# Inner products of each strip ahead of the outer ones, and one shifted input copy loaded from DRAM

## Chip, cores and metric

The kernel runs on one core of one Trainium2 chip. The metric is the device time of one launch in microseconds. The program is written with a scheduling layer: it allots the buffers and puts each engine's instructions in a fixed order when the program is built.

## What is computed

`reference` has two layers on an input of 4 images, 96 channels, 128 x 128 pixels. The first is a state-space block and isn't touched here. The second is an attention convolution:

```python
xr, x1, x2 = _relu_split_norm(x, sc1, sc2, res_coef, nc1, nc2)
# _attn_conv(x1, x2, aw1, aw2, aw3):
key = _unfold_nonoverlap(_conv2d(x1, aw1, pad), K)      # 3 x 3 convolution, 96 -> 96
qry = _unfold_nonoverlap(_conv2d(x2, aw2, pad), K)
attn = softmax(einsum('bckl,bqkl->bqck', key, qry) / sqrt(C * kk))
value = _conv2d(x1, aw3, pad)
y1 = _layer_norm(per image: _conv2d(value, attn))       # the attention is a 3 x 3 filter
y2 = _layer_norm(_conv2d(x2, w_conv2, 1)) * x1
out = x + xr + conv1x1([y1, y2], w_full) + b_full
```

So each image needs two pairs of 3 x 3 convolutions (the maps: `x1` with two filter sets, `x2` with two), a softmax, and a 3 x 3 convolution of the value with the attention filter.

## The kernel before

**Stages.** Up to about 3670 us the program does the state-space block and the maps of image 0. From there on it alternates, for images 0 to 3, between map stages (`attention` with `img.mapped` false, images 1 to 3) and value stages (all four images). The image is cut into strips of 12 rows (`AR`), eleven in all. Beside this main stream runs a light one: the norm and split of the next image and the output of the image before. `co_run` interleaves the two in the order of emission by costs that the generators yield.

**A convolution as products.** Along a row, four output pixels are made from six input planes (a minimal filtering scheme with the points 0, 1, -1, 2, -2 and infinity), so a strip needs six matrix products, numbered 0 to 5. Products 1 to 4 are the inner ones, 0 and 5 the outer ones. Planes are stored in DRAM in that form (`x1p`, `x2p`, `vp`), and loaded pair by pair: `PAIRS` (L1361) says which two planes make a tile, and the order of the tiles. The contraction runs over 96 channels x 3 rows. It is cut into three parts:

- `ya` (L1910): a loaded tile of 128 partitions, 96 channels of the upper row and the last 32 channels of the next one; eight buffers, three tiles a strip, loaded two strips ahead (`load`, L1898).
- `yb` (L1937): 64 channels shifted by one row on partitions 0 to 63, and by two rows on 64 to 127. Both halves are ScalarE copies of `ya` (L1938), three tiles of two copies for each strip, four buffers, made one strip ahead (`turn`, L1926).
- `yc` (L1918): the last 32 channels by two rows for products 1 and 3. The other products read theirs out of `ya`.

`products` (L1456) issues TensorE's work. `main(to, i)` puts the parts `ya` and `yb` of product i into PSUM (L1477), `rest` adds the 32-channel parts (L1492). A PSUM tile `two` holds two products; the pool has three buffers of two banks, and the transposes (L1770) and the key-query products (L1645) of the map stages use the same three. The order of one call is: main of 0 and 5 into one tile, `rest`, `outer`; main of 1, 3, 2, 4 into two tiles, `rest`, `sums`. After each `main` one entry of the list `fill` is called (a `yb` copy, a load, or both), then `later.tick()` emits what was put off.

`outputs` (L1531) makes the evacuation. `outer` copies the outer tile to SBUF on ScalarE (`ends`, L1550, two buffers). `sums` copies the tile of products 1 and 3 (`odd`, also L1550, one buffer). One tick later `combined` runs on VectorE: four sums and differences of the odd tile with the second tile (L1564 to L1567: two into `wide` in SBUF, two in place in PSUM), then four outputs (L1572) and, between them, the addition of `ends` (L1570). The second tile is read until the last of these.

A call for 128 output channels has 384 columns for a product. In a map stage each strip has, for each of the two inputs, such a call and one in which two half strips of 64 output channels stand side by side; in a value stage a strip has one call of 96 output channels. That is 132 + 44 = 176 calls and 110 strips of inputs.

At the end of a map stage `weights` (L1683) works off the last transposes and makes the softmax. The last call of `products` is held back and drawn from it piece by piece (`self.rest`): three pieces before the last transposes, two beside the softmax, the others after it.

Of the kernel before, what the change touches and what calls it, by code (L numbers as in the profile page):

```python
# [9 lines left out]
F32 = mybir.dt.float32  # L10
BF16 = mybir.dt.bfloat16
AF = mybir.ActivationFunctionType
ALU = mybir.AluOpType
# [58 lines left out]
def kernel(  # L72
# [1287 lines left out]

    PAIRS = ((0, 5), (1, 3), (2, 4))  # L1361
    PAIR = {i: k for k, pair in enumerate(PAIRS) for i in pair}
# [93 lines left out]
    def products(ps, jobs, ws, later, evac, threes=False, fill=()):  # L1456
# [42 lines left out]

        outer, sums = evac  # L1500
        fill = iter(fill)
# [6 lines left out]
        a = pairs_of(ps)  # L1508
        to = {0: a[:, 0], 5: a[:, 1]}
        for i, _ in TWO:  # L1510
            main(to[i], i)
            beside()
            later.tick()
            yield 1.3 * share
        rest(1, TWO, to)
        outer(a)
        later.tick()
        yield 0.4 + 0.4 * share
        a, b = pairs_of(ps), pairs_of(ps)
        to = {1: a[:, 0], 3: a[:, 1], 2: b[:, 0], 4: b[:, 1]}  # L1520
        for i, _ in FOUR:
            main(to[i], i)
            beside()
            later.tick()
            yield 1.3 * share
        rest(0, FOUR, to)
        sums(a, b)
        later.tick()
        yield 0.4 + 0.6 * share

    def outputs(pool, m, n, parts, later, then):  # L1531

        got = []

        def at(v, k):
            if isinstance(v, list):
                return v[k]  # L1540
            if len(v.shape) == 4:
                return v[:, :, k]
            return v.rearrange("p h (t k) -> p h t k", k=TW)[:, :, :, k]

        def rows(v):
            return v.rearrange("p (h t) -> p h t", t=TN)

        def copy_of(x, name, bufs):
            t = pool.tile([128, 2, AR * TN], F32, name=name, bufs=bufs)[:m, :, :n]
            nc.scalar.copy(t, x[:m, :, :n])  # L1550
            return t

        def outer(c):
            later(lambda: got.append(copy_of(c, "ends", 2)))

        def sums(a, b):
            def first():
                t = copy_of(a, "odd", 1)
                later(lambda: combined(t))

            def combined(t):
                w = pool.tile([128, 2, AR * TN], F32, name="wide", bufs=1)[:m, :, :n]
                ends, v = got[0], b[:m, :, :n]
                nc.vector.tensor_sub(w[:, 1], t[:, 1], v[:, 1])  # L1564
                nc.vector.tensor_add(w[:, 0], t[:, 1], v[:, 1])
                nc.vector.tensor_sub(v[:, 1], t[:, 0], v[:, 0])  # L1566
                nc.vector.tensor_add(v[:, 0], t[:, 0], v[:, 0])  # L1567
                for k, j, f in ((1, 1, AA), (2, 0, AA * AA), (0, 0, 1.0), (3, 1, AA**3)):
                    if k == 0:
                        nc.vector.tensor_add(v, ends, v)  # L1570
                    for p, e, o in parts:
                        nc.vector.scalar_tensor_tensor(  # L1572
                            at(o, k), rows(w[p:e, j]), f, rows(v[p:e, j]), ALU.mult, ALU.add
                        )
                later(then)

            later(first)

        return outer, sums

# [11 lines left out]
    class Taps:  # L1592
# [4 lines left out]
        def __init__(self, ps, later, pool, slots, taps):  # L1597
            self.ps, self.later, self.pool, self.slots = ps, later, pool, slots
            self.taps = [(k, min(k + taps, KK)) for k in range(0, KK, taps)]
            self.sm = pool.tile([C, KK, C], F32, name="sm")  # L1600
            self.rings = [pool.tile([128, 3, slots, PW], F32, name=f"ring{i}") for i in range(2)]
            for t in self.rings:
                nc.gpsimd.memset(t[:, :, :, 0:1].rearrange("p r i w -> p (r i) w"), 0.0)
            self.groups, self.todo, self.rest = 0, [], ()

# [77 lines left out]
        def weights(self):  # L1683
# [3 lines left out]
            self.later.flush()  # L1687
            for _ in range(3):
                yield next(rest, 0.0)
# [13 lines left out]
            yield 4.0  # L1703
            for _ in range(2):
                yield next(rest, 0.0)
# [15 lines left out]
    class PairTaps(Taps):  # L1721
# [3 lines left out]
        def __init__(self, ps, later, pool):  # L1725
# [8 lines left out]
            for t in self.rings:  # L1734
                for j in range(TW):
                    nc.gpsimd.memset(t[:, :, :, JB * j + TN : min(JB * (j + 1), JW)], 0.0)
            self.todo, self.rest = [], ()

# [144 lines left out]
    class Attention:  # L1883
# [3 lines left out]
        def __init__(self, ps, p1, p2, pm):  # L1887
# [5 lines left out]
            for b in range(1, NB):  # L1893
                self.todo += [(b, m, c) for c in self.chunks for m in (0, 1)]
                self.todo += [(b, 2, c) for c in self.chunks]
            self.raw, self.cols, self.c = {}, {}, 0

# [28 lines left out]
        def turn(self, c):  # L1926
# [8 lines left out]
            def copy(h, k):  # L1935
                if h == 1:
                    yb.append(self.p2.tile([128, 2, AR * TN], F32, name="yb", bufs=4))  # L1937
                nc.scalar.copy(  # L1938
                    yb[k][64 * h - 64 : 64 * h, :, :n], ya[k][0:64, :, h * TN : h * TN + n]
                )  # L1940

            return [lambda h=h, k=k: copy(h, k) for k in range(3) for h in (1, 2)]

        def begin(self):
            for c in (0, 1):
                for k in range(3):
                    self.load(c, k)
            for f in self.turn(0):
                f()
# [748 lines left out]
```

## Time and profile before

| | |
|---|---|
| median of 3 runs | 6409.91 us (6400.53 to 6413.18) |
| profiled execution, its own time | 6409.68 us |
| its span | 6407.8 us |
| busy: PE, DVE, ACT, POOL | 5253.4, 4699.9, 3759.4, 3238.6 us |
| bytes moved by DMA | 1205.30 MB, mean 188 GB/s |
| from 3670 us on (2738 us): PE, DVE, ACT, POOL busy | 2301.2, 1997.1, 1454.8, 935.8 us |

PE is TensorE's matmul, PEld its weight load, DVE is VectorE, ACT ScalarE, POOL GpSimd, SP the engine that issues most DMAs. A row of the waits reads "engine, tile and line that waited <- engine, tile and line that it waited for: total us, times, longest us". A row of the groups gives line, engine, operation, output <- input, shape, count, then busy us and mean ns, and the idle time ahead of it with what ended it. A row of the stage table gives a stretch in us and, for each engine, its busy us in it with the count of instructions. PEclk is the granted share of TensorE's full clock.

### The profile page before, as it was taken

How to read it: one execution, taken by the hardware profiler on the slowest of the kernel's cores; microseconds unless marked ns; L12 is line 12 of the kernel's file. 1: busy time of each engine (PE TensorE's matmuls, PEld its weight loads, DVE VectorE, ACT ScalarE, POOL GpSimd, SP SyncE). 2: the span in 40 equal slices, each digit the busy share in tenths (PEclk: the TensorE clock that was granted, in tenths of full speed). 3: DMA queues.
4: the chain of work that ended last, by engine and by line, in shares of the span. 5: the costliest groups of instructions: out<-in, count | busy, mean ns of one | idle time of the engine just before them, and what ended most of it. 6: DMA issues, size and time to landing. Idle time of an engine off the chain costs nothing. (4 is left out here: it accounts for less than half of the span.)

```text
span 6407.8 us, 76468 instructions
## 1 busy us (share of the span) xinstructions
PE 5253.4 (82%) x23264; PEld 2254.8 (35%) x23264; DVE 4699.9 (73%) x7132; ACT 3759.4 (59%) x4770; POOL 3238.6 (51%) x2476
## 2 busy tenths in 40 slices
PE   6889988987888643989988588977888877889888
PEld 2333322322222111444433234345333444345553
DVE  4247878988989768989844686468774687988767
ACT  1247767787787666777622465466644665545642
POOL 1326757978879554979822234436304365022310
PEclk9899989998999765999999799989989888999989
DMA  6766777775675766676667686665776656967668
GB/s 155 175 160 189 198 199 199 214 221 163 198 202 171 202 183 207 196 213 179 182 185 195 166 228 163 195 169 156 214 199 184 175 149 165 245 167 180 191 168 221
DMA packets 897706, 1205.30 MB, mean 188 GB/s; under 512 B 230644, under 2 KB 745642, under 8 KB 884816
## 3 DMA queue, kind: packets, MB, share of 16 engines
q1 hardware_dynamic: 866640, 1145.36, 65.5%
q0 software_dynamic: 16336, 38.51, 2.3%
q10 hardware_dynamic: 14320, 16.54, 0.9%
q8 instruction: 187, 3.06, 0.2%
q14 instruction: 223, 1.83, 0.1%
HBM read 777.82 MB, written 345.62 MB: 175 GB/s over the span
## 5 line engine op out<-in xcount | busy, mean ns | idle before, releaser
L633 PE MATMUL bank<-y,wp 128*128 128x512 f32 (+3 forms) x3584 | 1310.9, 622 | 83.8 <-DMA y<-y 41.0
L866 POOL TENSOR_TENSOR y<-y,dl 128x1024 f32<-128x1024 f32 x384 | 1058.5, 2757 | 263.0 <-DVE dl L858 240.3
L833 POOL TENSOR_TENSOR dl<-dl,u 128x1024 f32<-128x1024 f32 x384 | 1008.8, 2627 | 253.1 <-ACT dA L809 121.1
L854 DVE TENSOR_TENSOR_SCAN dA<-dA,pBC 128x512 f32<-128x512 f32 x768 | 981.6, 1278 | 30.7
L2169 PE MATMUL bank<-y,wn 128*64 128x384 f32 (+5 forms) x2408 | 680.1, 507 | 58.3 <-DMA y<-x1d 34.1
L1477 PE MATMUL two<-ya,wd 128*64 128x192 f32 (+3 forms) x2376 | 582.2, 414 | 174.0 <-ACT odd L1550 65.1
L633 PEld LDWEIGHTS bank<-y,wp 128*128 128x128 f32 (+3 forms) x3584 | 456.2, 168 | 749.3 <-issue 651.1
L858 DVE TENSOR_TENSOR dl<-dA,pBC 128x512 f32<-128x512 f32 x768 | 528.5, 688 | 255.8 <-PE pBC L747 183.8
L747 PE MATMUL pBC<-xr,wbc 60*128 60x512 bf16 (+1 forms) x1536 | 457.8, 404 | 311.5 <-DVE dA L854 239.1
L1938 ACT COPY yb<-ya 64x768 f32<-64x768 f32 (+1 forms) x660 | 537.7, 815 | 195.5 <-PE two L1477 113.8
L676 ACT ACTIVATE dl<-pd,dtb 128x512 f32<-128x512 f32 x768 | 485.5, 684 | 187.9 <-PE pd L747 171.5
L1477 PE MATMUL two<-yb,wd 128*64 128x192 f32 (+3 forms) x2376 | 559.0, 400 | 4.0 <-ACT yb L1938 4.0
L837 DVE TENSOR_TENSOR pBC<-dl,pBC 128x512 f32<-128x512 f32 x768 | 527.5, 687 | 8.8 <-POOL dl L833 7.8
L2169 PEld LDWEIGHTS bank<-y,wn 128*64 128x64 f32 (+3 forms) x2408 | 310.3, 169 | 357.2 <-issue 186.2
L809 ACT ACTIVATE dA<-dl,negA 128x1024 f32<-128x1024 f32 x384 | 420.3, 1141 | 2.3
L1477 PEld LDWEIGHTS two<-ya,wd 128*64 128x64 f32 (+1 forms) x2376 | 262.2, 165 | 370.9 <-ACT odd L1550 75.0
L676 ACT ACT_TABLE_LOAD x248 | 318.2, 1283 | 91.9 <-PE pd L747 79.7
L747 PEld LDWEIGHTS <-wbc 60*128 60x128 bf16 (+1 forms) x1536 | 103.1, 96 | 752.1 <-issue 739.3
L1477 PEld LDWEIGHTS two<-yb,wd 128*64 128x64 f32 (+1 forms) x2376 | 289.7, 167 | 150.5 <-issue 42.1
L1477 PE MATMUL two<-ya,wa 128*96 128x384 f32 (+1 forms) x528 | 231.2, 521 | 72.9 <-DMA ya<-vp 27.0
L1550 ACT COPY odd<-two 128x384 f32<-128x384 f32 (+5 forms) x176 | 115.8, 658 | 291.3 <-PE two L1492 179.1
L1406 POOL TENSOR_TENSOR pl<-x 96x256 f32<-96x256 f32 (+3 forms) x396 | 275.2, 710 | 0.0
(322 smaller groups left out, 9105.4 us busy)
## 6 DMA issues: line engine op xcount, KB each, us to landing
u<-zb SPq DMA_DIRECT2D x192, 1024.0 KB
yms<-y SPq DMA_DIRECT2D x96, 512.0 KB
xn<-xnew SPq DMA_DIRECT2D x128, 384.0 KB
ya<-vp SPq DMA_DIRECT2D x120, 336.0 KB
y<-y SPq DMA_DIRECT2D x128, 258.2 KB
zb<-z SPq DMA_DIRECT2D x64, 512.0 KB
y<-yms SPq DMA_DIRECT2D x64, 512.0 KB
ya<-x1p SPq DMA_DIRECT2D x90, 336.0 KB
```

Of the source, the lines that this page charges most:

```text
L633: nc.tensor.matmul(blocks(pz[p:e]), lhsT=ws[k][:, d, c : c + e - p], rhs=window(ys[k], at, d, n), start=(i == 0), stop=(i == len(terms) - 1),)
L676: nc.scalar.activation(dst, src, AF.Softplus, bias=bias)
L747: nc.tensor.matmul(p, lhsT=w[rows], rhs=xr[rows, at : at + CH], start=True, stop=True)
L809: nc.scalar.activation(live[m]["dA"], live[m]["dl"], AF.Exp, scale=negA[:, g % 3, k : k + 1])
L833: nc.gpsimd.tensor_mul(t, t, u_view(n))
L837: nc.vector.tensor_mul(p, live[n]["dl"][:, bass.ts(half, CH)], p)
L854: nc.vector.tensor_tensor_scan(h, h, p, init, ALU.mult, ALU.add)
L858: nc.vector.tensor_mul(live[n]["dl"][:, sl], live[n]["dA"][:, sl], live[n]["C", half])
L866: nc.gpsimd.tensor_add(v, v, t.rearrange("p (a b) -> p a b", b=W))
L1477: nc.tensor.matmul(of(to[p:e], r), lhsT=w[:, i, c : c + e - p], rhs=tiles(t[k][PAIR[i]][:, SLOT[i]], o, r), start=(k == 0), stop=False,)
L1938: nc.scalar.copy(yb[k][64 * h - 64 : 64 * h, :, :n], ya[k][0:64, :, h * TN : h * TN + n])
L2169: nc.tensor.matmul(pc[p:e, :n].rearrange("p (h w) -> p h w", w=W), lhsT=w[:, c : c + e - p], rhs=v[:, :, 0:W], start=(i == 0), stop=(i == ...
```

## The change

Three things change. (1) In `products` the four inner products come first; the second tile is requested only when product 2 needs it; the outer ones follow. `PAIRS` is put in the same order, so that the inner planes are loaded and copied first. (2) `outer` and its copy go. `sums` writes all four sums and differences to one SBUF tile (`sums`, twice the size of `wide`) with two instructions of full width and makes outputs 1 and 2; `ends`, called after the outer products, adds the outer tile in PSUM to the sums and makes outputs 3 and 0. (3) In the room of the `ends` tiles a tile `yd` (two buffers) takes the place of the third `yb` tile: its partitions 64 to 127 are loaded from DRAM two strips ahead (`load_direct`), the other half is still a ScalarE copy. `yb` has three buffers now. The pieces of the held-back call are split (2, 3) around the softmax, where they were (3, 2). In the built program ScalarE has 440 `yb` and 110 `yd` copies (660 `yb` before) and no `ends` copies, VectorE has 352 instructions fewer, SP 110 DMAs more; TensorE's count is the same.

```diff
-    PAIRS = ((0, 5), (1, 3), (2, 4))
+    PAIRS = ((1, 3), (2, 4), (0, 5))
...
-        outer, sums = evac
+        sums, ends = evac
...
+        a = pairs_of(ps)
+        to = {1: a[:, 0], 3: a[:, 1]}
+        for i, _ in FOUR:
+            if i == 2:
+                b = pairs_of(ps)
+                to |= {2: b[:, 0], 4: b[:, 1]}
+            main(to[i], i)
+            beside()
+            later.tick()
+            yield 1.3 * share
+        rest(0, FOUR, to)
+        sums(a, b)
+        later.tick()
+        yield 0.4 + 0.6 * share
         a = pairs_of(ps)
         to = {0: a[:, 0], 5: a[:, 1]}
         for i, _ in TWO:
...
         rest(1, TWO, to)
-        outer(a)
+        ends(a)
         later.tick()
         yield 0.4 + 0.4 * share
-        a, b = pairs_of(ps), pairs_of(ps)
-        to = {1: a[:, 0], 3: a[:, 1], 2: b[:, 0], 4: b[:, 1]}
-        for i, _ in FOUR:
...
+        def out(k, x, f, y):
+            for p, e, o in parts:
+                nc.vector.scalar_tensor_tensor(
+                    at(o, k), rows(x[p:e]), f, rows(y[p:e]), ALU.mult, ALU.add
+                )
...
             def combined(t):
+                u = pool.tile([128, 2, 2, AR * TN], F32, name="sums", bufs=1)[:m, :, :, :n]
+                v = b[:m, :, :n]
+                nc.vector.tensor_sub(u[:, :, 1], t, v)
+                nc.vector.tensor_add(u[:, :, 0], t, v)
+                out(1, u[:, 1, 1], AA, u[:, 0, 1])
+                out(2, u[:, 1, 0], AA * AA, u[:, 0, 0])
+                made.append(u)
...
+        def ends(c):
+            def closed():
+                if not made:
+                    later(closed)
+                    return
+                u, v = made[0], c[:m, :, :n]
+                nc.vector.tensor_add(v, u[:, 0], v)
+                out(3, u[:, 1, 1], AA**3, v[:, 1])
+                out(0, u[:, 1, 0], 1.0, v[:, 0])
                 later(then)
...
             def copy(h, k):
-                if h == 1:
-                    yb.append(self.p2.tile([128, 2, AR * TN], F32, name="yb", bufs=4))
+                if k == 2:
+                    yb.append(self.direct.pop(c))
+                elif h == 1:
+                    yb.append(self.p2.tile([128, 2, AR * TN], F32, name="yb", bufs=3))
...
-            return [lambda h=h, k=k: copy(h, k) for k in range(3) for h in (1, 2)]
+            fill = [lambda h=h, k=k: copy(h, k) for k in range(3) for h in (1, 2)][:5]
+            return [*fill, lambda: self.load_direct(c + 1)]
+
+        def load_direct(self, c):
...
+            i0, i1 = PAIRS[2]
+            t = self.direct[c] = self.p2.tile([128, 2, AR * TN], F32, name="yd", bufs=2)
+            src = src_of[0:64, slice(i0, i1 + 1, i1 - i0), r0 + 2 : r0 + 2 + r]
+            nc.sync.dma_start(
+                t[64:128, :, : r * TN], src.rearrange("c i h t -> c i (h t)")
+            )
```

More of the change, by code (lines that the diff above doesn't have):

```diff
@@ L1515, in products @@
         rest(1, TWO, to)
-        outer(a)
+        ends(a)
         later.tick()
         yield 0.4 + 0.4 * share
-        a, b = pairs_of(ps), pairs_of(ps)
-        to = {1: a[:, 0], 3: a[:, 1], 2: b[:, 0], 4: b[:, 1]}
-        for i, _ in FOUR:
[L1522 to L1529, printed above, removed]
     def outputs(pool, m, n, parts, later, then):
-        got = []
+        made = []
         def at(v, k):
@@ L1546, in rows @@
             return v.rearrange("p (h t) -> p h t", t=TN)
[L1548 to L1554, printed above, removed]
+        def out(k, x, f, y):
[3 more added lines that the diff above has]
+                )
@@ L1556, in sums @@
         def sums(a, b):
             def first():
-                t = copy_of(a, "odd", 1)
+                t = pool.tile([128, 2, AR * TN], F32, name="odd", bufs=1)[:m, :, :n]
+                nc.scalar.copy(t, a[:m, :, :n])
                 later(lambda: combined(t))
             def combined(t):
-                w = pool.tile([128, 2, AR * TN], F32, name="wide", bufs=1)[:m, :, :n]
-                ends, v = got[0], b[:m, :, :n]
-                nc.vector.tensor_sub(w[:, 1], t[:, 1], v[:, 1])
@@ L1565, in combined @@
[L1565 to L1574, printed above, removed]
+                u = pool.tile([128, 2, 2, AR * TN], F32, name="sums", bufs=1)[:m, :, :, :n]
@@ new lines, in combined @@
+                v = b[:m, :, :n]
[4 more added lines that the diff above has]
+                made.append(u)
+            later(first)
+        def ends(c):
[7 more added lines that the diff above has]
+                out(0, u[:, 1, 0], 1.0, v[:, 0])
@@ L1575, in combined @@
                 later(then)
-            later(first)
-        return outer, sums
+            later(closed)
+        return sums, ends
     def by_threes(v, r):
@@ L1603, in __init__ @@
                 nc.gpsimd.memset(t[:, :, :, 0:1].rearrange("p r i w -> p (r i) w"), 0.0)
-            self.groups, self.todo, self.rest = 0, [], ()
+            self.groups, self.todo, self.rest, self.held = 0, [], (), (3, 2)
         def flat(self, m):
@@ L1687, in weights @@
             self.later.flush()
-            for _ in range(3):
+            for _ in range(self.held[0]):
                 yield next(rest, 0.0)
@@ L1703, in weights @@
             yield 4.0
-            for _ in range(2):
+            for _ in range(self.held[1]):
                 yield next(rest, 0.0)
@@ L1736, in __init__ @@
                     nc.gpsimd.memset(t[:, :, :, JB * j + TN : min(JB * (j + 1), JW)], 0.0)
-            self.todo, self.rest = [], ()
+            self.todo, self.rest, self.held = [], (), (2, 3)
         def flat(self, m):
@@ L1895, in __init__ @@
                 self.todo += [(b, 2, c) for c in self.chunks]
-            self.raw, self.cols, self.c = {}, {}, 0
+            self.raw, self.cols, self.direct, self.c = {}, {}, {}, 0
         def load(self, c, k):
@@ L1940, in copy @@
                 )
-            return [lambda h=h, k=k: copy(h, k) for k in range(3) for h in (1, 2)]
+            fill = [lambda h=h, k=k: copy(h, k) for k in range(3) for h in (1, 2)][:5]
+            return [*fill, lambda: self.load_direct(c + 1)]
+        def load_direct(self, c):
+            if c >= len(self.todo):
+                return
+            b, m, (r0, r) = self.todo[c]
+            src_of = (imgs[b].x1p, imgs[b].x2p, imgs[b].vp)[m]
+            r = (r + 2) // 3 * 3
+            i0, i1 = PAIRS[2]
[4 more added lines that the diff above has]
+            )
         def begin(self):
@@ L1947, in begin @@
                     self.load(c, k)
+            self.load_direct(0)
             for f in self.turn(0):
```

## The prediction

> **What bounds the kernel now.** I read the stage table first, then TensorE's waits, then the groups of instructions, and the timeline last. The change touches only the last part of the run, from 3670 us on, where `Attention` works: eleven strips for each value product (four stages) and eleven strips for each pair of maps (three stages). Busy time by stage (the columns are PE, PEld, DVE, ACT, POOL, the granted TensorE clock, the DMA share and GB/s):
>
> ```profile
> 3670.00:3830.00 160.00, 125.80 (x402) 52.04 (x403) 135.02 (x222) 107.82 (x141) 61.80 (x83) 0.88 0.88 234
> 3830.00:4650.00 820.00, 686.31 (x4004) 359.02 (x4002) 563.39 (x1144) 474.30 (x665) 360.90 (x519) 0.92 0.67 180
> ...
> 4900.00:5480.00 580.00, 469.29 (x2913) 265.79 (x2913) 419.41 (x836) 335.47 (x478) 277.12 (x401) 0.88 0.64 170
> 5480.00:5640.00 160.00, 139.71 (x443) 58.49 (x443) 141.06 (x180) 81.21 (x94) 0.00 (x0) 0.94 0.87 234
> 5640.00:6190.00 550.00, 485.56 (x3223) 288.39 (x3219) 418.56 (x665) 288.14 (x363) 166.34 (x239) 0.94 0.66 176
> ```
>
> TensorE is busy 81 to 88% of the map stages (second, third and last row); no other engine passes 77% there. Over all 2738 us PE is busy 2301 and idle 437. Its work is one ordered stream, so a microsecond of its idle time is a microsecond of the run unless another wait takes its place. What ended that idle time:
>
> ```profile
> PE two L1477 <- ACT odd L1550: 80.3, 37, 10.1
> PE two L1477 <- ACT kt L1775: 43.0, 31, 3.7
> PE two L1477 <- ACT ends L1550: 28.4, 19, 3.4
> PE two L1477 <- DMA ya<-vp: 27.0, 1, 27.0
> PE two L1645 <- ACT odd L1550: 25.0, 15, 6.3
> ...
> PE two L1477 <- ACT yb L1938: 23.4, 15, 3.6
> PE two L1645 <- DVE ring L1572: 19.0, 10, 5.6
> ...
> PE two L1770 <- ACT odd L1550: 13.6, 9, 3.3
> ```
>
> Read these as waits for a PSUM buffer: a matmul that starts a new `two` tile waits until the tile that last held the slot has been read out. Summed by releaser over all rows: `odd` copies 119 us in 61 waits, `ends` copies 30, `kt` copies 49, VectorE's last outputs (L1572) 47, `yb` copies 23 (an input, not a slot). By stage `odd` is 49 us in 3830 to 4650, 44 in 4900 to 5480, 9 in 5640 to 6190 and 18 in the four value stages together.
>
> The copies take under 0.8 us; they cost TensorE because ScalarE comes to them late:
>
> ```profile
> ACT ends L1550 <- PE two L1492: 232.4, 79, 7.8
> ...
> ACT odd L1550 <- PE two L1492: 179.1, 52, 9.5
> ...
> ACT yb L1938 <- PE two L1477: 113.8, 63, 11.9
> ```
>
> ScalarE executes in order. While it stands at an `ends` or a `yb` copy whose TensorE work isn't done, nothing behind it runs, and it then also has the norm and split instructions of the next image ahead of the `odd` copy. At 4304.2 to 4310.5 one such case is open in the timeline: TensorE idles 6.3 us, while ScalarE works through two activations and two `yb` copies before `odd` at 4310.02, and VectorE still holds the previous product's second tile until its L1572 of 4310.89.
>
> [...] `plv<-diff` (L1406, both inputs SBUF, 96x256) has a median of 414 ns but a mean of 558 and a maximum of 2782, while L1572, with one PSUM input, has 548 and at most 557 for the `ring` shape. [...] after the idle 27.04 us at 3681.63 pairs of matmuls start 1.28 us apart, later 0.64. [...]
>
> **Part by part.** The sum is made against the profiled execution: span 6407.8, its own time 6409.68, the median of the runs 6409.91; they differ by less than I can resolve, so I count from 6410.
>
> *Copies removed (ScalarE).* 176 `ends` copies, busy 115.8 us, and one `yb` copy in six: 110 x 0.815 us = 90 us. 206 of 1455 us in the window. ScalarE is not the bound, so this is worth only what it takes off TensorE's waits. Its 232 us of standing at `ends` go too, and the wait of the third pair's copy for a slot.
>
> *VectorE.* Four differences and sums of half width become two of full width: [...] Against that, two of the four output instructions (L1572) now read two SBUF tiles. The bound below is 0 (no GpSimd at work, as in 5480 to 5640, POOL 0.00); above, the mean excess of L1420, mean 688 less median 417 = 0.27 us, on 132 map products x 2 = 71 us. I take 0.2 us, 53 us. VectorE is a wash; nothing gained or lost on the path.
>
> *PSUM slots.* This decides. In the order of the built program (map stages) the old sequence is ends-tile, odd-tile, second tile, then transposes: 26 of 44 second tiles start on the slot whose `ends` copy was issued just two matmul groups before, and the tile behind the four inner products often takes the odd slot with only a transpose or product of 2 to 3 us between. In the new one, for 40 of 44 products of the first map stage, the odd slot is next taken by a transpose or a product of transposes that stands behind the two outer products (about 3.3 us in these stages), and the second tile is released after two VectorE instructions (1.9 us), not nine (about 5.3 us). But the outer tile is now released by VectorE (add and two outputs, 0.96 + 2 x 0.55 = 2.1 us), not by ScalarE in 0.8 us, and second tiles come round sooner. In the value stages 10 of 11 outer tiles take the odd slot directly, so a wait of one copy stays.
> Map stages: `odd` and `ends` are 117 us of waits; I let a third remain: -76. Value stages: 32 us become 38 direct reuses x 0.65 us = 25: -7. `yb`: half of 23: -10. Waits for VectorE: 47 become 60: +13. Bounds: nothing of the 172 us goes (and +40 for VectorE comes), or all of it.
>
> *The new load.* 110 loads of 64 x 2 x 384 floats, 197 KB, 21 MB. The page's first queue took 65.5% of 16 x 6407.8 us for 866640 packets, 77.5 ns each; at one packet a row (an estimate) a load is 128 x 77.5 / 16 = 0.62 us of all engines. In a map stage that is hidden under a share of 0.67; in a value stage 11 x 0.62 = 6.8 us are 4 points on 0.88. The tile is filled two strips ahead, so its cover is a whole strip (12 us and more); if the cover were gone each value stage would lose up to 7 us, 27 in all. The load waits on SP until the outer products of strip c, which still read the slot that strip c + 2 is to have, are done. Behind it stand the stores of `oc`, the next `ya` loads and the light work's loads. SP already stands 231 us at the `yc` load (L1921) for the same place in TensorE's stream; with the inner products first that wait ends earlier, and the new one ends where the old one did. Between 0 and 2 us each (231/110); I take +8 us for loads and queue together.
>
> *Order of the rest.* In `weights` the held-back product now gives three pieces to the softmax gap instead of two, and one accumulating tile stays in PSUM during the last transposes: within 3 us either way, three times, 0. At the end of the run the last evacuation is four VectorE instructions shorter: 3.5 us of the chain 6356.2 to 6360.2 shrink by about 2: -2.
>
> *Clock.* From the stage table idle 11.7% goes with clock 0.94, 16.3% with 0.92, 19.1% with 0.88. 74 us less idle on 1950 us of map stages are 4 points; bounds 0 and 4 points of clock on 1641 busy us (60 us, if clock followed idle one for one). I take -11.
>
> Sum: -76 - 7 - 10 + 13 + 8 - 2 - 11 = -85 us: 6325.
>
> **Rivals.** (1) *The lateness is not ScalarE's.* What delays `odd` is the light work's chain: ScalarE waits 75 us for VectorE's `half`, 54 for `mq`, 75 for TensorE's `bank`. Then `odd` stays late, only `ends` (-30) and `yb` (-10) go and new waits give 20 back: 6390. For it: the 10.1 us maximum. Against: most waits are 1 to 3 us, in reach of the added slack.
> (2) *VectorE becomes the releaser that is late* (slower). Two of three tiles of a product are now freed by VectorE, the busiest evacuator (337 of 420 us in 5060 to 5480), whose queue is shared with the split. At 4303 us it was a whole product behind. Savings before new waits are 106 us; so it decides from 106/132 = 0.8 us of new wait per map product, against 47/176 = 0.27 now. At 1.2 us: 158 - 106 = +52: 6462. For it: slots of second tiles are reused 3 tiles later where it was 5. Against: release work falls from 5.3 to about 2 us.
> (3) *All the slot waits go* and the clock follows: -172 - 40: 6200.
> (4) *The change doesn't do it*: excluded; the built program has 440 + 110 copies for 660, no `ends`, 110 new loads, and the same 16953 TensorE instructions.
>
> **How the numbers follow.** Forecast (6255 to 6385) 0.60; rival 3 and anything below 6255 0.10; rival 1 (6385 to 6423) 0.13; rival 2 above 6423 0.17. A difference under about 0.2% (13 us) can't be told from none, so of rival 1 a third counts as faster. Faster 0.74, same 0.09, slower 0.17. The range 6250 to 6435 leaves out about 0.1 on each side.
>
> **What would show it.** Right: no `ends`; TensorE's waits for `odd` near 50 us; its waits for VectorE outputs near 60; VectorE's busy time within 20 us; ScalarE about 206 us less; PEclk up 1 to 2 points in the map stages. Wrong: waits for `sums`, `two` or outputs of VectorE above 150 us (rival 2), `odd` still over 100 (rival 1), or waits for DMA `yd` at all.

## The result

The changed kernel takes 6489.39 us (median of 6 runs, 6485.9 to 6507.95) against 6400.65 us of the kernel before (6 runs, 6377.87 to 6413.18): a ratio of 1.0159, 95% interval 1.0141 to 1.0177. It is slower by about 1.6%, where the forecast said faster by 1.3%, and it lies above the range. (The two medians alone give 1.0139, 89 us: the kernel before took 6401 us here and 6396 to 6412 us beside the runs below, so a difference between runs that were not made together is uncertain by some 0.2%.) The profiled execution took 6487.49 us, its span is 6485.7 us; the clock is 0.897 where it was 0.902.

Of the busy time, the forecast was nearly right: VectorE 4690.2 us (9.7 less), ScalarE 3560.2 us (199 less), GpSimd 3250.7 us. TensorE is the one that differs: 5296.3 us for the same instructions (43 more). The stage table, from the first product of each stage to the first of the next (columns as in the forecast: PE, PEld, DVE, ACT, POOL, clock, DMA share, GB/s); here the second map stage, the value stage after it, the last map stage and the sum of all seven, of the kernel before:

```profile
4632.20:5430.00 797.80, 647.66 (x3678) 335.34 (x3676) 555.34 (x1043) 421.54 (x582) 329.99 (x458) 0.88 0.64 174
5430.00:5612.10 182.10, 164.56 (x503) 67.10 (x503) 153.94 (x198) 93.74 (x109) 5.70 (x16) 0.95 0.90 241
5612.10:6195.30 583.20, 510.19 (x3313) 300.04 (x3314) 446.31 (x706) 301.88 (x378) 166.34 (x239) 0.94 0.67 178
...
sum 2726.20, PE 2301.19 PEld 1180.58 DVE 1993.62 ACT 1453.38 POOL 934.62; mean PE 328.74 PEld 168.65 DVE 284.80 ACT 207.63 POOL 133.52
```

and of the changed one:

```profile
4641.10:5478.70 837.60, 666.85 (x3678) 340.23 (x3676) 557.51 (x944) 376.39 (x511) 329.99 (x462) 0.86 0.62 170
5478.70:5672.80 194.10, 173.13 (x503) 68.86 (x503) 154.67 (x189) 81.47 (x94) 4.88 (x11) 0.92 0.88 236
5672.80:6269.20 596.40, 522.40 (x3317) 306.90 (x3318) 424.64 (x616) 253.84 (x309) 162.09 (x239) 0.92 0.65 177
...
sum 2817.60, PE 2347.23 PEld 1197.33 DVE 1985.12 ACT 1255.22 POOL 946.38; mean PE 335.32 PEld 171.05 DVE 283.59 ACT 179.32 POOL 135.20
```

All seven stages together are 91 us longer. That is 13 more than the span's 78, because the first value stage began 13.5 us earlier than before and ended at the same time. TensorE is busy 46 us longer and idle 45 us longer (470 against 425). The clock records of the two traces have only two values, full and half; in this part the clock stood at half for 575 us, where it had been 487. The second map stage alone gives 40 us. TensorE's waits over the whole of this part, in the changed kernel:

```profile
PE two L1477 <- DVE own L1553: 41.9, 22, 7.7
PE two L1477 <- issue: 39.6, 22, 5.3
PE two L1477 <- ACT odd L1560: 38.9, 34, 3.3
...
PE two L1477 <- DMA yd<-x2p: 26.2, 4, 10.0
...
PE two L1653 <- ACT odd L1560: 24.4, 8, 13.0
PE two L1778 <- DVE sums L1567: 22.8, 11, 6.0
PE two L1778 <- ACT odd L1560: 19.8, 13, 6.7
PE two L1477 <- DVE sums L1567: 19.4, 10, 5.0
...
PE two L1477 <- DVE ring L1553: 15.0, 9, 3.3
```

Of ScalarE's releases, `odd` has gone from 119 to 83 us, `ends` from 30 to 0, the input copies from 23 to 9. But VectorE's releases (`sums`, and the tiles of outputs `own` and `ring`) are 110 us where they were 47, the load is waited for 26 us, and 48 us have no releaser that the profile shows ("issue", here and in a smaller row), against 3 before. The waits have not gone; they have changed their owner.

### The profile page after: what moved, and what is told of

It is laid out like the page before. It is cut to its first block, busy times and chain, and to the rows that moved or that the text cites. A ratio compares the mean times of both kernels' runs of the same rounds, so it can differ in the third digit from the quotient of the medians.

```text
span 6485.7 us, 76017 instructions
## 1 busy us (share of the span) xinstructions
PE 5296.3 (82%) x23264; PEld 2268.6 (35%) x23264; DVE 4690.2 (72%) x6780; ACT 3560.2 (55%) x4484; POOL 3250.7 (50%) x2476
## 5 line engine op out<-in xcount | busy, mean ns | idle before, releaser
L1477 PE MATMUL two<-ya,wd 128*64 128x192 f32 (+3 forms) x2376 | 587.9, 417 | 134.7 <-ACT kt L1783 34.8
L1948 ACT COPY yb<-ya 64x768 f32<-64x768 f32 (+1 forms) x440 | 358.3, 814 | 154.0 <-PE two L1477 74.2
L1477 PEld LDWEIGHTS two<-ya,wd 128*64 128x64 f32 (+1 forms) x2376 | 268.8, 168 | 326.9 <-issue 129.2
L1477 PE MATMUL two<-yb,wd 128*64 128x192 f32 (+2 forms) x1584 | 379.4, 406 | 0.4 <-ACT yb L1948 0.4
L1477 PE MATMUL two<-ya,wa 128*96 128x384 f32 (+1 forms) x528 | 237.0, 534 | 110.5 <-DMA wa<-watd 27.2
L1566 DVE TENSOR_TENSOR sums<-odd,two 128x384 f32<-128x384 f32 (+5 forms) x176 | 137.1, 779 | 216.0 <-ACT odd L1560 187.0
```

Of the source, the lines that this page charges most:

```text
L1477: nc.tensor.matmul(of(to[p:e], r), lhsT=w[:, i, c : c + e - p], rhs=tiles(t[k][PAIR[i]][:, SLOT[i]], o, r), start=(k == 0), stop=False,)
L1948: nc.scalar.copy(yb[k][64 * h - 64 : 64 * h, :, :n], ya[k][0:64, :, h * TN : h * TN + n])
```

## Taking the change apart

Each run is given by its ratio to the kernel before in the runs of the same chip. The changed kernel is 1.0159; 0.0010 is 6.4 us. First the load and the outer tile. In the first run ScalarE makes all six copies again:

```diff
-            fill = [lambda h=h, k=k: copy(h, k) for k in range(3) for h in (1, 2)][:5]
-            return [*fill, lambda: self.load_direct(c + 1)]
+            return [lambda h=h, k=k: copy(h, k) for k in range(3) for h in (1, 2)]
...
-            self.load_direct(0)
```

> The changed kernel with all six shifted copies on ScalarE again and no load of its own for the third pair; inner products first and the uncopied outer tile stay. If VectorE as the late releaser costs the time (theory A), nothing is gained back: 6475 to 6500 us, with some 110 us of TensorE's waits on VectorE's sums and outputs. If the load does (theory B: 26 us of TensorE's waits for it, 48 us of issue, a fuller SP queue), most of the 89 us come back: 6400 to 6430. If it is the order of the pieces (theory C), 6475 to 6500 as well.

1.0058 (1.0045 to 1.0070), 6450.72 us. The time lies in none of the expected ranges. Without the load the kernel is 0.0101 faster, 65 us by the ratios (39 between the medians, but the kernel before took 6411 us beside this run and 6401 beside the changed kernel); the rest of the change costs 0.6%. Neither theory A nor B holds alone. Next, in addition, the outer tile is copied by ScalarE:

```diff
         def ends(c):
+            t = pool.tile([128, 2, AR * TN], F32, name="ends", bufs=1)[:m, :, :n]
+
+            def copied():
+                nc.scalar.copy(t, c[:m, :, :n])
+                later(closed)
...
-                u, v = made[0], c[:m, :, :n]
+                u, v = made[0], t
...
-            later(closed)
+            later(copied)
```

> As the run without the load, and the outer tile is copied to SBUF by ScalarE again, so that ScalarE and not VectorE releases its slot; inner products are still first, and the second tile is still released after two full-width VectorE sums. Theory A, if the outer tile is the slot that matters: 6390 to 6430. Theory B: the same as without the load, within 15 us, or slower by the copies. Theory C (the order as such): as slow as the changed kernel or slower, 6480 to 6520.

1.0045 (1.0028 to 1.0061), 6440.04 us: not to be told from the run above. The value stages do show what the forecast's second rival named. In the third of them, without the load:

```profile
PE two L1477 <- DVE own L1553: 14.9, 9, 2.6
PE two L1477 <- ACT odd L1560: 3.9, 4, 1.2
```

and with the outer tile copied by ScalarE:

```profile
PE two L1477 <- ACT ends L1578: 6.6, 7, 2.0
PE two L1477 <- ACT yb L1952: 5.1, 4, 1.3
```

Over the four value stages the wait for VectorE's `own` is 42 us in the first run, under 1 us in the second and 3 us in the kernel before, and the four are 687, 662 and 669 us long. So there VectorE as the releaser of the outer tile seems to cost what ScalarE's copy didn't; the two programs also differ in the order of their instructions, which matters below, so this is a reading. The map stages are 2077, 2079 and 2057 us long. But the profiled run of the second kernel is its fastest by 22 us (6416.25; the others 6438.9 to 6453.81), and the median keeps 11 us of the gain.

Then the load on the side of the kernel before, and its control, which makes the room for it by one buffer less for `ends` (the load's lines are those of the change):

```diff
-            later(lambda: got.append(copy_of(c, "ends", 2)))
+            later(lambda: got.append(copy_of(c, "ends", 1)))
```

> The kernel before with only the load of the third pair's shifted copy to a tile of its own added (yb in 3 buffers, ends in 1 for the room); outer products first, outer tile copied by ScalarE, sums as they were. Theory B: 6450 to 6490, with waits of TensorE for the load. Theory A and C: 6380 to 6405, since 90 us of ScalarE's work go and nothing else does.

> The kernel before with one buffer for the copied outer tile where it had two: the control for the runs that need the room. All theories: within 15 us of before, 6390 to 6420; if it is slower by more, the runs with one buffer have to be read against this one.

1.0202 (1.0182 to 1.0222) with the load, 1.0149 (1.0129 to 1.0168) without: with the load the kernel is 36 us slower here too, though 110 copies go. Both are slower than any theory expected. The control was the surprise, 95 us for one buffer. ScalarE's waits give it a plain reason, a copy that stands until VectorE has added the last one:

```profile
ACT odd L1550 <- PE two L1492: 241.3, 74, 8.0
ACT ends L1550 <- DVE two L1570: 184.2, 54, 12.8
```

It is not needed for most of the loss, as a run with both buffers below shows.

## Is it the load's traffic?

Four smaller edits of the changed kernel and its relatives. In the first the load is made in the map stages alone; in the value products ScalarE fills the same tile with the copy `last`:

```diff
+            def end():
+                if self.todo[c][1] == 2:
+                    last()
+                self.load_direct(c + 1)
...
             t = self.direct[c] = self.p2.tile([128, 2, AR * TN], F32, name="yd", bufs=2)
+            if m == 2:
+                return
```

> The changed kernel with the third pair's load made only in the map stages; in the value products ScalarE copies it into the same tile, so the buffers are the same. If the load costs what its bytes cost on the DMA engines of the value stages (44 loads, 24 us between the runs with and without the load): 6460 to 6470, with the value stages 20 to 27 us shorter together than in the changed kernel and the map stages as there. If it costs through the SP queue or TensorE's waits for the tile in the map stages: 6480 to 6495. If VectorE as the late releaser were behind all of it: no change, 6485 to 6495.

1.0142 (1.0116 to 1.0168). The value stages of the profiled run are 21 us shorter together (691 us), as expected, but the map stages are 21 us longer, though nothing was edited in them (the profiled run is the slowest of the five, 11 us above their median). Next, the closing addition one step later, and the numbers of held pieces put back:

```diff
-            later(closed)
+            later(closed, 1)
```

```diff
-            self.todo, self.rest, self.held = [], (), (2, 3)
+            self.todo, self.rest, self.held = [], (), (3, 2)
```

> The changed kernel with the closing addition and its two outputs put into VectorE's stream one step later, so that VectorE stands less at it while TensorE still works on the outer products. If standing at the closing addition (81 us) is what delays what VectorE does behind it: faster by 10 to 30 us, 6460 to 6480. If what decides is when the outer tile comes free: slower by 10 to 40, 6500 to 6530. If neither lies on the path: within 10 us of 6489.

> The changed kernel with the numbers of held pieces around the softmax of the second class put back from (2, 3) to (3, 2). The forecast put this part at nothing within 3 us; all theories: within 10 us of 6489. If it is off by more, the placing of single pieces alone moves the time by so much, and differences of that size between other kernels are not to be explained.

1.0140 (1.0117 to 1.0162) and 1.0177 (1.0153 to 1.0200). Neither is to be told from 1.0159, though the second median, 6507 us, misses the expected 10 us around 6489. Moving the closing addition (L1580), at which VectorE stands 81 us, brings nothing, and the held pieces are worth nothing that shows.

Then the load without any use: six copies on ScalarE as in the first run, and a load of the same bytes into a tile that nobody reads, in the value stages alone (the lines below) or in the map stages alone (`m == 2` there). The tile takes the room that the first run leaves free:

```diff
+            if m != 2:
+                return
...
+            t = self.p2.tile([128, 2, AR * TN], F32, name="yd", bufs=1)
```

> The changed kernel without its load, six copies on ScalarE (6451), and a load of the same bytes in the value stages alone into a tile that nobody reads: nothing waits for it, and no buffer or copy changes. If what the load costs in the value stages is the traffic on the DMA engines: 6465 to 6480, the value stages 15 to 25 us longer together. If it was a wait or a buffer: 6445 to 6456.

> The same with the unread load in the map stages alone. If traffic is behind the 20 to 50 us that the map stages lose with the load: 6465 to 6490. If it was the waits for the tile, the three buffers of yb or the placing: 6445 to 6460, as the DMA share is 0.62 to 0.68 there.

In the value stages, where the DMA engines were busiest (share 0.80 to 0.87, with the load 0.86 to 0.92), it costs nothing: 1.0069 (1.0050 to 1.0088) against 1.0058. In the map stages, with a share of 0.6 to 0.7, it costs 0.8%: 1.0137 (1.0115 to 1.0159), above even the range that was expected of traffic. That is the wrong way round for traffic, and nothing waits for this load.

What it does change is found in the built programs. Counted from them, without the load itself, 707 of VectorE's instructions and 480 of TensorE's stand out of the order of the kernel without load once the unread load is in the map stages (the fewest that would have to be moved to restore it). With the unread load in the value stages, which cost nothing, they are 72 and 42; with the changed kernel's own load, 730 and 598. On TensorE an instruction of the light work (norm, split and output of other images) stands on average 14 matmuls of the main stream later, and 40 or more for one in twenty; with the changed kernel's own load it is the same 14. The scheduling layer chose another order because the load was there; that it goes by its own estimate of when each instruction can start is likely, but not shown.

## Order against load

So the order was taken from one kernel and imposed on the other: for each engine, a list of the positions of all instructions from the end of the state-space block on, and a dependency without a semaphore from each to the next.

```diff
+    def pin(keep):
+        for text in PINNED.values():
+            raw = zlib.decompress(base64.b85decode(text))
+            at = 0
+            row = []
+            for d in struct.unpack(f"<{len(raw) // 2}h", raw):
+                at += d
+                row.append(keep[at])
+            for a, b in zip(row, row[1:]):
+                assert a.engine == b.engine
+                tc.add_manual_dep(
+                    b,
+                    a.name,
+                    mybir.DependencyInfo(
+                        mybir.DependencyClass.NoSync, mybir.DependencyReason.DATA
+                    ),
+                    reason="order of another build",
+                )
...
     drain(last.after(psl))
+    keep = [i for j, i in enumerate(traced()) if j >= begun and j not in set(marks)]
+    pin(keep)
```

`marks` holds the loads, which stay free (in the list for the third run below, the 110 copies that the load replaces are left out).

> The kernel with the unread load in the map stages (6496), but with the instructions of every engine in the order that the scheduling layer chose for the kernel without that load (6451); only the loads stand between SP's others. If the load costs through the order that it makes the layer choose: 6440 to 6462. If the bytes, or SP's time for them, cost the 45 us: 6485 to 6500.

> The kernel without the load (6451), with the instructions of every engine in the order that the layer chose for the kernel with the unread load in the map stages (6496). If the order costs the 45 us: 6482 to 6500, with no load at all. If the bytes do: 6440 to 6460.

| | no load | unread load in the map stages |
|---|---|---|
| order chosen without the load | 1.0058 (1.0045 to 1.0070) | 1.0073 (1.0051 to 1.0095) |
| order chosen with the load | 1.0125 (1.0104 to 1.0146) | 1.0137 (1.0115 to 1.0159) |

Down a column the order changes and costs 0.0067 and 0.0064, some 42 us; along a row the load changes and costs 0.0015 and 0.0012, less than the intervals can tell from nothing. Two of the four kernels carry an imposed list and two don't, so the list itself costs nothing that shows either. For this load the order is the cause, and it works with no load in the program at all.

The traces show one place. In the second map stage, TensorE's waits for `odd` at a key-query product (L1653; L1854 and L1855 in the two kernels with a list, whose lines are moved by it). First the old order, without and with the load:

```profile
PE two L1653 <- ACT odd L1560: 9.9, 5, 5.7
```

```profile
PE two L1854 <- ACT odd L1761: 8.6, 4, 4.8
```

and the new order without a load:

```profile
PE two L1855 <- ACT odd L1762: 15.9, 2, 12.5
```

A single wait of 12.5 us. The changed kernel has the same hole, 13.0 us, at 5093.9 us; it is 13.0 in the kernel with the unread load as well, and there is none like it in the three that have the old order (the third of them follows below), where the longest of these waits is 5.7 us. The timeline around it in the changed kernel, ScalarE's lines and the matmul that waited (start, duration, instruction):

```profile
5094.32 0.82 ACT L1948 COPY yb<-ya 64x768 f32<-64x768 f32 x1
5095.04 1.06 ACT L1154 ACTIVATE xz<-xr 96x1024 f32<-96x1024 f32 x1
...
5096.09 1.23 ACT L1147 ACTIVATE xr<-xn,shift,rstd 96x1024 f32<-96x1024 f32 x1
...
5098.60 1.24 ACT L1147 ACTIVATE xr<-xn,shift,rstd 96x1024 f32<-96x1024 f32 x1 [1.18 <-DMA xn<-xnew]
...
5104.12 1.23 ACT L1147 ACTIVATE xr<-xn,shift,rstd 96x1024 f32<-96x1024 f32 x1
...
5106.39 0.46 ACT L1560 COPY odd<-two 128x384 f32<-128x384 f32 x1
...
5106.90 1.43 PE L1653 MATMUL two<-kt 90*96 90x96 f32 x7 [13.01 <-ACT odd L1560]
```

TensorE's inner products end at 5091.9 and the outer ones behind them at 5093.9, where its idle time begins. The `odd` copy of 0.46 us that frees the inner products' slot runs at 5106.39, behind ten activations of the next image's norm (L1147, L1154; eight of them begun after 5093.9) and two input copies. This is the lateness that the forecast had read from the kernel before, in a place where the layer had not put it before. Such holes need no load: 330 us later the kernel in the new order without one is idle 12.3 us again, until two `yb` copies end that stood behind the split's activations. The old order has a hole of its own in this stage, 11.9 us at a product of the light work in all three of its kernels, so an order is not told good or bad by one hole.

> The changed kernel as it is, its load read by TensorE and 110 copies fewer on ScalarE, but in the order that the layer chose for the same kernel without the load (6451). If the 38 us between the two are the order: 6430 to 6458, the copies saved adding a little. If they are the load itself, its wait or its buffers: 6478 to 6495.

1.0081 (1.0058 to 1.0104), 6459.59 us, a shade above the range expected of the order: the changed kernel itself, with its load read and its copies saved, but in the order chosen without the load. The order is worth 0.0078, 50 us, of its 1.59% (30 us between the medians, with the kernel before at 6412 beside this run and 6401 beside the other). And the load with its 110 saved copies is worth nothing that shows (1.0081 against 1.0058, with overlapping intervals), although TensorE waits 23 us for it in this order too. Its second map stage and the sum of its seven stages:

```profile
4652.50:5475.30 822.80, 645.35 (x3673) 332.67 (x3672) 562.91 (x941) 377.47 (x512) 334.66 (x468) 0.88 0.65 174
...
sum 2772.70, PE 2307.99 PEld 1186.77 DVE 1991.52 ACT 1258.16 POOL 945.76; mean PE 329.71 PEld 169.54 DVE 284.50 ACT 179.74 POOL 135.11
```

Against the changed kernel in its own order that is 45 us less, and only 6 of them are idle time (465 against 470); 39 are busy time of the same matmuls. By the clock records the clock stood at half for 510 us, not 575. So the holes are what the eye finds, but here the order costs through the clock more than through the idle time in sum. In all three pairs of one program in an old and a new order (without load, with the unread load, the changed kernel) the new one costs 13 to 17 us in the second value stage, 15 to 28 in the second map stage and 16 to 25 in the third, and gains 7 to 18 in the first map stage.

> The kernel before, with two buffers for the copied outer tile as it is, but in the order that the layer chose for one buffer (6506). If the 95 us of that run are the copies' wait for the one buffer: 6400 to 6425. If they are the order that the layer chose when it saw that wait: 6480 to 6510. In between, both.

1.0130 (1.0109 to 1.0151). The kernel before, every buffer as it was, is 83 us slower in the order that the layer chose for one `ends` buffer. In that order the one buffer adds only the other 12 us of the control's 95, less than the intervals can tell from nothing; what one buffer costs in the old order was not run.

## What is left

The changed kernel in the better order is still 0.8% slower than before, and without the load 0.6%. Three runs had been made to find that part, before the order was known as a cause: sums at full width with the outer products first (one `ends` buffer), and the order of the products alone, with two buffers for the copied outer tile and with one.

```diff
-                nc.vector.tensor_sub(w[:, 1], t[:, 1], v[:, 1])
-                nc.vector.tensor_add(w[:, 0], t[:, 1], v[:, 1])
-                nc.vector.tensor_sub(v[:, 1], t[:, 0], v[:, 0])
-                nc.vector.tensor_add(v[:, 0], t[:, 0], v[:, 0])
+                nc.vector.tensor_sub(u[:, :, 1], t, b[:m, :, :n])
+                nc.vector.tensor_add(u[:, :, 0], t, b[:m, :, :n])
```

> The kernel before with one buffer for the copied outer tile, and with the sums and differences at full width into a tile of their own, so that the second tile is released after two VectorE instructions; outer products first, as before. It is to be read against the kernel before with one such buffer (6506) and against the kernel with inner products first and the outer tile copied by ScalarE (6440), which has the same operations and tiles in the other order. If the contention of two SBUF inputs costs the time: slower than 6506, 6515 to 6540. If it is the early release that helps: 6460 to 6490, and then the order is worth what is left to 6440. If the order alone decides: 6495 to 6515.

For the order of the products, against the changed kernel: the operations of the kernel before are kept, and `ends` has two buffers, then one.

```diff
-                u = pool.tile([128, 2, 2, AR * TN], F32, name="sums", bufs=1)[:m, :, :, :n]
...
+                w = pool.tile([128, 2, AR * TN], F32, name="wide", bufs=1)[:m, :, :n]
...
+                made.append((w, v))
...
+            t = pool.tile([128, 2, AR * TN], F32, name="ends", bufs=2)[:m, :, :n]
+
+            def copied():
+                nc.scalar.copy(t, c[:m, :, :n])
+                later(closed)
```

> The kernel before with the order alone changed: inner products first, and all operations, tiles and buffers as before (the outer tile copied by ScalarE, two buffers for it, four half-width sums and differences, the second tile worked on in PSUM and held until the outer products are in). If the order as such is good and the full-width sums are what costs (so far 6506 to 6533 between the two runs with outer products first): 6360 to 6395. If holding the second tile over the outer products costs more than the order gives: 6420 to 6460. If the order is worth nothing with two buffers: within 12 us of before, 6400.

> The same with one buffer for the copied outer tile; the fourth corner of a square with the runs outer first and half width (6506), outer first and full width (6533), inner first and full width (6440), all with one buffer. If the two edits just add: 6410 to 6420. If the full-width form pays only because it frees the second tile early when inner products come first: 6445 to 6480.

1.0214 (1.0189 to 1.0239), 1.0095 (1.0071 to 1.0119) and 1.0079 (1.0058 to 1.0100). Each is a program with an order of its own, and a new order alone was worth 0.7% to 1.3% above. So no mechanism can be read from them, not even that inner products first is better with one buffer (1.0079 against 1.0149). They are inconclusive.

The last two runs tried to hold the light work in its old place: each of its instructions stands behind as many main matmuls as in the kernel before, and the main stream keeps the order that it had without the load.

> The changed kernel with its own operations, load and tiles; the main stream's instructions stand in the order of the kernel without the load, and every instruction of the light work stands where the layer put it in the kernel before, counted by TensorE's matmuls of the main stream. If all that the change costs is the place of the light work: 6395 to 6420. If the evacuation as rewritten (VectorE frees two tiles of three, two SBUF inputs) costs the rest of the time, as the run in the order without the load (6460) suggests: 6440 to 6465.

> The kernel with inner products first and the outer tile copied by ScalarE, without the load (6440), with the light work where the kernel before has it. If VectorE as the releaser of the outer tile is what is left of the cost: 6395 to 6425, 25 us or more below the run above, most of it in the value stages. If it is the full-width sums and the order of the products: 6435 to 6460, within 15 us of the run above. Below 6395 it would beat both kernels.

1.0243 (1.0228 to 1.0259) and 1.0297 (1.0281 to 1.0314): far slower than either theory said. A place that fits one main stream doesn't fit another, so this was no neutral ground, and the two runs tell nothing on the evacuation. They do widen the scale: the changed kernel's operations take 6460, 6489 and 6566 us in three orders, more than the whole change moved.

The trace without the load shows the same exchange as the changed kernel: `odd` waits 72 us and no `ends`, together 77 us less than before, but 96 us of waits for VectorE's `own`, `sums` and `ring` where there were 47, and 30 us of "issue" where there were 3. This exchange doesn't hang on the order: in all eleven kernels in which VectorE frees the outer tile TensorE waits 85 to 118 us for VectorE's outputs and sums, and in all nine in which ScalarE's copy frees it 20 to 56 us (and 30 to 117 us for `ends`). What it is worth in time is not shown by an experiment: the two kernels that differ in this point (and in their order) are 1.0058 and 1.0045. What part of the 0.6% is order stays open, and so does what the "issue" waits are.

## The forecast, step by step

| step | forecast, us | measured in the waits or runs |
|---|---|---|
| `odd` and `ends`, map and value stages | -83 | -66 (119 and 30 to 83 and 0) |
| input copies | -10 | -15 (23.4 to 8.9) |
| waits for VectorE's tiles | +13 | +63 (47 to 110) |
| waits with no releaser (issue) | not thought of | +46 (3 to 48) |
| load and queue | +8 | +26 of waits; 30 to 50 us by the order that came with it |
| order of the rest | 0, within 3 | see below |
| tail | -2 | not to be seen in the last stage (212.5 to 216.5 us) |
| clock | -11 | TensorE busy 46 us longer, 88 us more at half clock |

*What was right.* ScalarE's lateness as the cause of the `odd` waits, and that they would shrink; VectorE's and ScalarE's busy time. The two sums and differences of full width (L1566, L1567) are busy 273.7 us where the four of half width (L1564 to L1567 of the kernel before) were 328.7: 55 us less over 176 products, 312 ns each. Outputs with two SBUF inputs take 616 ns in the mean, those with one 549 (`ring<-sums` and `ring<-sums,two`, 128x384), and for `oc` 641 against 343. Over the window that is 41 us by the rows of all shapes (120 x 67 ns, 76 x 83, 60 x 298, 60 x 98 and 12 x 210), near the 53 that were set down. In the third value stage, where GpSimd is busy for only 4.9 us, the two forms of `own` (96x384) take 549 and 544 ns, against 711 and 628 over the window, so the lower bound of nothing was right as well. That GpSimd's work is the cause was the forecast's assumption; the traces show no more than these times.

*The step that failed first* is "The new load", and with it "Order of the rest". The load was priced by its bytes, at an estimated 128 packets each (the two pages differ by 15840 packets in the first queue, 144 for each load), and by what stands behind it on SP, 0 to 2 us each. For traffic the price was fair: in an unchanged order the unread load costs 8 to 10 us, less than the intervals tell from nothing. TensorE's waits for the tile, 23 to 26 us, were not in it; the forecast had named any such wait as a sign that it was wrong, and it is the only one of its three signs that came. But above all the text took the order of the instructions as given except where the diff moves them, and asked only where the held-back pieces go. The order is an output of the build: 66 loads that nobody reads put 707 of VectorE's instructions in another place and cost 42 us. The comparison of the built programs was at hand, and was used for the counts of instructions and the PSUM slots, not to ask what the light work had in front of it now.

*The second, and by size the larger,* is the term of VectorE's waits, 13 against 63, and with it the waits with no releaser, put at nothing, 46. They don't come from the new order: with the order of the kernel without load the changed kernel still has 106 us of waits for VectorE and 27 of "issue", and there it is 52 us slower than before, where 85 us faster was forecast. The second rival named this: two of three tiles of a product freed by VectorE, behind the light work. It set the turning point at 0.8 us of new wait for each map product. Measured are 23 us more over the 44 value products (0.5 each) and 40 over the 132 map products (0.3): below the point, so rival 2 alone would not have made the kernel slower. One case shows the mechanism. VectorE's timeline in the changed kernel:

```profile
5396.19 0.76 DVE L1566 TENSOR_TENSOR sums<-odd,two 128x576 f32<-128x576 f32 x1 [0.95 <-ACT odd L1560]
5396.86 0.70 DVE L1413 SCALAR_TENSOR_TENSOR diff<-half 96x528 f32<-96x528 f32 x1
5397.48 3.65 DVE L1414 SCALAR_TENSOR_TENSOR diff<-half 96x512 f32<-96x512 f32 x1
5401.06 1.51 DVE L1418 TENSOR_TENSOR diff<-half 96x528 f32<-96x528 f32 x1
5402.49 0.74 DVE L1567 TENSOR_TENSOR sums<-odd,two 128x576 f32<-128x576 f32 x1
```

The second tile is free after two instructions of 0.75 us, as the forecast counted. But three instructions of the split stand between the two, one of them 3.65 us long where the mean of its 44 like it is 1.18, and TensorE is idle 6.0 us until 5403.38. Two instructions in the source were not two in the stream.

*The clock* had the wrong sign. The forecast let it follow idle time, a seventh of a microsecond of busy time for each. In the four runs of the table the new order does go with 22 and 20 us more idle time (446 to 468, 448 to 468) and with 37 and 28 us more busy time of the same matmuls. But over all runs the sum of idle time doesn't tell the busy time: the changed kernel in the better order has 465 us idle and 2308 busy, the order of the products alone with one buffer 466 and 2288, the unread load in the value stages 437 and 2336. What goes with the busy time in most kernels is the time at half clock while TensorE works: 371 us before, 425 in the changed kernel, 366 in the same kernel in the better order. In the trace of before the clock record is at half from 3639.05 to 3686.83 us, and pairs of matmuls start 1.28 us apart in it; at full clock, from 3689.11 us on, they start 0.64 to 0.65 apart (L1477, 128x384). If, as an estimate from that, half of the time at half clock is counted as lost, the busy time left is 2116, 2135 and 2125 us, nearly the same work (2115 to 2142 us in eighteen of the twenty kernels; 2095 and 2183 in the other two, not explained). What brings the clock down was not shown: the half clock just named begins 15.5 us ahead of the idle 27.04 us that the forecast saw before its slow pairs.

*The rivals.* The first (the light work's chain delays `odd`) has its place in the 13 us hole. The second is seen at 0.3 to 0.5 us a product, below the 0.8 that it needed. That the order would be redrawn was no rival at all; it should have been one, with both signs.

## What to carry to other kernels

Where a layer orders the instructions, a small edit can redraw much of the order, and the edit's size doesn't tell how much: the same unread load put 707 of VectorE's instructions in another place in the map stages and 72 in the value stages. The new orders that came with it and with one buffer less moved the time by 0.7% and 1.3%. Before a small gain or loss is put down to a mechanism, compare the built orders, and impose the order of one kernel on the other; four runs in a square (order by edit) tell the two apart. An order belongs to its stream, though: a place for side work that fits one kernel cost 1.6% in another (1.0081 to 1.0243).

## What was not expected of the hardware

Load on the DMA engines was nearly free where it looked dearest: 44 loads of 192 KB in stages with a share of 0.8 to 0.87 raised it to 0.86 to 0.92 and cost nothing that shows (1.0069 against 1.0058). And TensorE's busy time is no constant of the work: the same matmuls of the seven stages took 2301 us before, 2347 in the changed kernel, 2308 in that kernel in another order and 2359 in the control with one buffer; the time at half clock while it worked was 371, 425, 366 and 433 us.
